# Moving the last FFN pair, the first-layer chunks and the value projections between the head slots of a transformer block kernel

## The chip, the cores and the metric

The kernel runs on one NeuronCore of a Trainium2 chip. Its engines run side by side, each in its own program order, and wait for one another by semaphores: TensorE (PE, with its weight loads shown apart as PEld), VectorE (DVE), ScalarE (ACT), GpSimd (POOL) and SyncE (SP), which here issues the DMA transfers. The metric is the device time of one execution in microseconds; less is better.

## What is computed

The input x has 16 batches of 512 tokens with 256 features. Each batch is normalised, and attention and a feed-forward network with weights of +1 and -1 are added to x:

```python
xn = _layernorm(x, axis=-1)
# attention, 8 heads of width 128
q = einsum('bim,mhd->bhid', xn, wq); k = einsum('bim,mhd->bhid', xn, wk)
v = einsum('bim,mhd->bhid', xn, wv)
q = rope(q); k = rope(k)
s = einsum('bhid,bhjd->bhij', q, k) / 128
s = s - 1e30 * mask                       # causal, i < j
o = einsum('bhij,bhjd->bhid', softmax(s), v)
attn = einsum('bhid,hdm->bim', o, wo)
# FFN, 512 -> 1024 -> 1024 -> 256
h = concatenate([xn, -xn], axis=-1)
h = relu(s0 * (h @ where(k0, 1, -1))) * 2
h = relu(s1 * (h @ where(k1, 1, -1))) * 2
ffn = s2 * (h @ where(k2, 1, -1))
out = x + attn + ffn
```

## The kernel before

The work is cut into 128 slots, one per batch and head; slot g has batch b = g // 8 and head h = g % 8. Below, "slot h" means the slot of head h in each batch. The slots are a software pipeline. In slot g the kernel computes the four score rows of head g with their softmax (`score_row`, L553), projects q and k of head g + 1 (`project_qk`, L508), applies the probabilities of head g - 1 to the values (`attend`, L618) and projects the result of head g - 2 to the output (`project_o`, L652).

A score row takes this way: PE multiplies (L558), DVE adds the mask and finds the least value (L561), ACT takes the exponential and its sum (L566), DVE the reciprocal (L568), POOL scales the row (L569). At the end of a slot `turn` (L573) lets DVE transpose the four rows in blocks (z, L578); SP stores them to a bounce buffer in DRAM (L335) and loads them back in another order as pT (L341, four transfers), which `attend` of the next slot reads. POOL also rotates q and k: multiplication of the swapped halves swq and swk with the sine table (L440) and addition into qT and kT (L442). The next slot's first score row waits for kT, the last POOL instruction of the chain.

The products of the projections and of the second FFN layer use seven products in the place of eight for a 2 by 2 split (`seven_products`, L464). They need differences of the operand's blocks: T1 to T4 of xn (`make_ts`, L398) and of the first layer's result (`add_h0`, L704, four POOL subtractions L708 per chunk). The two PSUM tiles pa and pb of such a product are accumulated in steps; ACT copies their state between steps to ca, cb and cu (L482, L487, L491), and the later steps on the same tile wait for these copies.

The FFN of a batch has three parts. The first layer (`ffn0`, L675) makes eight 128-row tiles, two for each of four chunks. ACT writes relu of it to h0r (L699). `split_h0` (L710) splits a chunk in a high part h0h, cast by ACT (L713), and a low remainder h0l, subtracted by DVE (L714), once for the plain blocks (PLAIN) and once for the four differences (SUMS). The second layer (`ffn1`, L718) runs in four pairs of seven products with 56 matmuls each, over weights w1 that lie in DRAM as two parts: part 0 (A11, A12, S1, A22; 1024 KB) is read by the first two steps of a pair and part 1 (S2, S4, A21; 768 KB) by the rest. From the second batch on both are loaded again for each pair (`load_w1`, L166). h0r of chunks 0 and 2 lies in the buffer of part 0, h0r of chunks 1 and 3 in that of part 1, so a chunk and a weight part wait for each other. The third layer (`ffn2`, L749) adds a finished pair to y, the PSUM sum that also takes the outputs of the heads.

The values v are projected in four steps a batch (`project_v`, L531): two groups of four heads with two token parts each.

Before the change the special slots are these. Slot 0 runs the last pair (3) of the batch before, and at its end chunks 0 and 1 of the first layer. Slot 1 runs chunks 2 and 3 and value step (0, 1). Slot 2 runs value step (1, 0), the third layer of pair 3 of the batch before, the `store` (L657) of that batch and the normalisation of the next batch's x. Slots 3, 5 and 6 run pairs 0, 1 and 2, and the slots after them the third layer of these (slots 4, 6 and 7). The next batch's x is transposed in slot 3, sent to DRAM in slot 4 (`carry_xn_out`) and brought back in slot 5 (`carry_xn_back`). Value step (1, 1) is in slot 4 and step (0, 0) of the next batch in slot 7.

The order of instructions on PE, SP and POOL is the program order, written by hand in `slot`, `slot_of_head_0` and `slot_of_head_1`: a generator such as `project_qk` stops at each `yield`, and `some(gen, n)` and `rest(gen)` place its next steps between the score rows. The order on DVE and ACT is set by a planner, which `behind` ties to a slot's rows. `begin` (L829) issues a slot's transfers on SP.

## Time and profile before

| what | value |
|---|---|
| median of two runs | 2250.07 us (2248.95 to 2251.2) |
| profiled execution, own time | 2253.46 us |
| its span, first to last instruction | 2251.6 us |
| PE, DVE, ACT, POOL busy | 2109.5, 1526.3, 1365.8, 1280.9 us |
| mean granted TensorE clock | 0.984 |
| DMA traffic | 455.55 MB, mean 202 GB/s |
| mean slot lengths, slots 0 to 7, batches 2 to 14 | 19.7, 20.6, 15.9, 18.9, 14.1, 16.0, 18.0, 14.7 us |
| one batch | 137.9 us |

The span is the time from the first to the last instruction of the one execution that was traced. A slot's length is the time from its first score matmul (128x128, L558) to that of the next slot, read from PE's timeline. Busy time of PE counts matmuls with modelled ends, so a busy PE may still run below its peak. In the waits of PE the two largest totals are 47.3 us for the copy ca_v in 42 places and 29.5 us for the load of w1 in 17 places.

### The profile page before, as it was taken

To read this page: it belongs to the slowest core of one execution; us is meant where nothing else is said; L and a number is where in the kernel's file an instruction comes from. 1 tells how busy PE (TensorE), PEld (TensorE's weight loads), DVE (VectorE), ACT (ScalarE), POOL (GpSimd) and SP (SyncE) were. 2 spreads that over 40 slices of the span, in tenths; PEclk is the share of its full clock that TensorE was granted. 3 is DMA by queue.
4 is the path that set the end of the run, shared out by engine and by line. 5 is a ranking of instruction groups with operands and counts; after the bars stand their busy time and mean duration, and the time that the engine had idled before them with its cause. 6 is when DMAs were issued, how large, how long until landed. Compare 5 with 4: busy or idle time off the path is not lost.

```text
span 2251.6 us, 34771 instructions
## 1 busy us (share of the span) xinstructions
PE 2109.5 (94%) x11392; PEld 1792.9 (80%) x11392; DVE 1526.3 (68%) x3774; ACT 1365.8 (61%) x2884; POOL 1280.9 (57%) x1332
## 2 busy tenths in 40 slices
PE   7899999989999899998999989999899999989998
PEld 4677878878788787787878878788787877878787
DVE  7877667676666766667667676766767666676664
ACT  6656565565656656566566566656556565565663
POOL 6546456465555656456465565655556456465652
PEclk9999999999999999999999999999999999999999
DMA  4684957749477584775847658486684957748575
GB/s 146 216 259 128 277 159 223 235 140 264 140 237 229 150 255 143 236 216 158 271 146 234 215 163 274 131 258 188 181 252 128 281 160 224 237 143 250 161 223 161
DMA packets 214596, 455.55 MB, mean 202 GB/s; under 512 B 30992, under 2 KB 150800, under 8 KB 206224
## 3 DMA queue, kind: packets, MB, share of 16 engines
q1 hardware_dynamic: 213392, 452.42, 66.3%
q8 instruction: 91, 1.49, 0.3%
q10 hardware_dynamic: 1024, 0.92, 0.1%
q14 instruction: 89, 0.73, 0.1%
HBM read 339.22 MB, written 114.03 MB: 201 GB/s over the span
## 4 chain that ended last, share of the span: by engine, by line
PE 67%; DVE 15%; ACT 6%; DMA 6%; issue 3%; POOL 1%; SPq 0%; ACTq 0%; DVEq 0%; POOLq 0%
PE pa_h L725 11%; PE y L644 11%; PE po L599 10%; PE pb_h L725 8%; PE s L558 7%; PE pa_qk L517 7%; PE pb_qk L517 6%; DMA w<-w_dram 5%; DVE h0l L714 4%; PE ph L692 3%; PE pa_v L541 3%; DVE z L578 2%; DVE p L561 2%; PE pb_v L541 1%; ACT h0r L699 1%
## 5 line engine op out<-in xcount | busy, mean ns | idle before, releaser
L569 POOL TENSOR_SCALAR p<-p,rl 128x128 f32<-128x128 f32 (+3 forms) x512 | 319.7, 627 | 594.6 <-DVE rl L568 593.1
L558 PE MATMUL s<-kT,qT 128*128 128x128 f32 (+3 forms) x1024 | 364.0, 437 | 1.7 <-DVE least L561 1.7
L566 ACT ACTIVATE p<-p,least 128x128 f32<-128x128 f32 (+3 forms) x512 | 287.9, 563 | 119.2 <-DVE least L561 113.7
L440 POOL TENSOR_TENSOR swq<-swq,sin_sb 128x512 f32<-128x512 f32 x127 | 192.1, 1513 | 270.2 <-ACT swq L435 268.4
L725 PE MATMUL pa_h<-h0h,w 128*128 128x256 f32 x1024 | 294.6, 322 | 33.5 <-DMA w<-w_dram 29.5
L599 PE MATMUL po<-pT,v 128*128 128x256 f32 (+1 forms) x1536 | 300.7, 345 | 2.9 <-DMA pT<-bounce_p 2.9
L599 PEld LDWEIGHTS po<-pT,v 128*128 128x128 f32 x1536 | 268.2, 191 | 34.4 <-issue 3.3
L561 DVE CUSTOM_DVE_ANT_0 p<-s,causal 128x128 f32<-128x128 f32 (+3 forms) x512 | 245.6, 484 | 71.3 <-PE s L558 68.1
L578 DVE STREAM_TRANSPOSE z<-p 128x128 f32<-128x128 f32 (+3 forms) x512 | 237.3, 489 | 52.2 <-POOL p L569 51.3
L708 POOL TENSOR_TENSOR h0r<-h0r 128x256 f32<-128x256 f32 x256 | 232.4, 933 | 53.9 <-ACT h0r L699 50.1
L725 PE MATMUL pa_h<-h0l,w 128*128 128x256 f32 x1024 | 257.1, 286 | 0.0
L644 PE MATMUL y<-wo,oT 128*128 128x256 f32 x1024 | 253.1, 392 | 0.0
L714 DVE TENSOR_TENSOR h0l<-h0r,h0h 128x1024 fp32r<-128x1024 f32 (+1 forms) x128 | 189.8, 1483 | 91.3 <-ACT h0h L713 91.2
L725 PEld LDWEIGHTS pa_h<-h0h,w 128*128 128x128 f32 x1024 | 196.9, 192 | 65.8 <-issue 16.1
L644 PEld LDWEIGHTS y<-wo,oT 128*128 128x128 f32 x1024 | 202.4, 199 | 30.4 <-issue 0.5
L725 PE MATMUL pb_h<-h0h,w 128*128 128x256 f32 x768 | 212.8, 313 | 0.0
L725 PEld LDWEIGHTS pa_h<-h0l,w 128*128 128x128 f32 x1024 | 198.0, 193 | 16.0 <-issue 15.2
L558 PEld LDWEIGHTS s<-kT,qT 128*128 128x128 f32 x1024 | 184.7, 193 | 21.5 <-DVE least L561 2.3
L626 ACT COPY oT<-po 128x512 f32<-128x512 f32 x127 | 74.5, 586 | 189.4 <-PE po L599 189.4
L725 PE MATMUL pb_h<-h0l,w 128*128 128x256 f32 x768 | 189.3, 283 | 0.0
L434 ACT COPY swq<-q 64x512 f32<-64x512 f32 x126 | 78.2, 621 | 175.5 <-DVE q L525 173.8
L442 POOL TENSOR_TENSOR qT<-qT,swq 128x512 f32<-128x512 f32 x127 | 168.8, 1329 | 10.0
(132 smaller groups left out, 4644.4 us busy)
## 6 DMA issues: line engine op xcount, KB each, us to landing
bounce_p<-z SPq DMA_DIRECT2D x128, 640.0 KB, 3.5
pT<-bounce_p SPq DMA_DIRECT2D x512, 160.0 KB, 4.0
w<-w_dram SPq DMA_DIRECT2D x60, 1024.0 KB, 6.8
w<-w_dram SPq DMA_DIRECT2D x120, 448.0 KB, 5.4
w<-w_dram SPq DMA_DIRECT2D x60, 768.0 KB, 8.5
wv<-wv_dram SPq DMA_DIRECT2D x30, 896.0 KB, 6.2
wo<-in_L_attn_wo_dram SPq DMA_DIRECT2D x128, 128.0 KB, 5.4
w<-w_dram SPq DMA_DIRECT2D x60, 256.0 KB, 7.1
```

The costliest lines, as they stand in the source:

```text
L440: engine.tensor_tensor(sw, sw, sin_sb, ALU.mult)
L517: nc.tensor.matmul(out_, w[:, place], of_xn(b, x), skip_group_check=True, **marks)
L558: nc.tensor.matmul(ps[:, :n], qT[:, ts(ic, P)], kT[:, :n], start=True, stop=True)
L561: reduced = nc.vector.tensor_tensor_reduce(out=p, in0=ps[:, :n], in1=causal[:, T - n :], scale=1.0, scalar=3e38, op0=ALU.add, op1=ALU.min, ...
L566: raised = nc.scalar.activation(p, p, AF.Exp, bias=least, scale=-1.0, accum_out=l)
L569: nc.gpsimd.tensor_scalar(p, p, rl, 1.0, ALU.mult, ALU.mult)
L578: behind(nc.vector.transpose(zs[:, :, block(ic, 0) : block(ic + 1, 0), :].rearrange("p j c a -> p c j a"), p.rearrange("p (c j a) -> p c j ...
L599: nc.tensor.matmul(po[:, (ics[0] - first) * P : (ics[-1] + 1 - first) * P], v[:, jc], pT[:, :, at[0] : at[-1] + 1 : max(at[-1] - at[0], 1) ...
L644: nc.tensor.matmul(ys[b][c // 2][:, c % 2, :], lhsT[:, ts(c, P)], rhs, start=(y_done[b][c] == 0 and c % 2 == 0), stop=(y_done[b][c] == N_Y ...
L708: nc.gpsimd.tensor_tensor(r[:, out_], r[:, p], r[:, q], ALU.subtract)
L714: behind(nc.vector.tensor_tensor(lo, r, hi.bitcast(F32), ALU.subtract), reduced)
L725: nc.tensor.matmul(out_, w1s[b, i, place][:, c], t[:, c, x], start=start and not c + n, stop=stop and c == NC - 1 and n == 1, skip_group_c ...
```

## The change

The last pair runs in slot 7 of its own batch, so that pairs are in slots 3, 5, 6 and 7 and the third layer always in the slot after. The first layer's chunks 0 and 1 run in slot 0 between the score rows, chunk 2 in slot 1 and chunk 3 in slot 2; their POOL differences now stand between the score rows too. The value steps are in slots 0, 1, 2 and 4. The store of a batch moves from slot 2 to slot 1. Normalisation, transposes, transfer out and transfer back of the next batch's x come a slot later (slots 3, 4, 5 and 6), its T differences are made in the second half of slot 6, and the load of x two batches on moves from slot 3 to slot 4. Part 0 of the first pair's weights is issued in the `turn` of slot 2 as before; part 1 is issued by `begin` of slot 3.

The diff:

```diff
--- before.py
+++ after.py
@@ -817,13 +817,14 @@
         nc.sync.dma_start(wv7_dram[gv], wv7s[0, gv])
 
 
+    PAIR_SLOTS = (3, 5, 6, 7)
+    assert NPAIR == len(PAIR_SLOTS)
+
     def pair_of(g):
 
         b, h = divmod(g, H)
-        if h == 0 and b:
-            return b - 1, NPAIR - 1
-        if h in (3, 5, 6) and b < B:
-            return b, (3, 5, 6).index(h)
+        if h in PAIR_SLOTS and b < B:
+            return b, PAIR_SLOTS.index(h)
         return None
 
     def begin(g):
@@ -843,12 +844,10 @@
             load_w2(*now)
         if b == B:
             return
-        if h in (4, 6, 7):
-            i = (4, 6, 7).index(h) + 1
-            if b == 0:
-                store_w1(i)
-            elif h != 6:
-                load_w1(b, i, 1)
+        if b == 0 and h in (4, 6, 7):
+            store_w1((4, 6, 7).index(h) + 1)
+        elif b and h in (3, 4):
+            load_w1(b, h - 3, 1)
         if b == 0:
             if g == 1:
                 store_wv7(0)
@@ -858,16 +857,15 @@
                 store_wv7(1)
             if h in (3, 4, 6):
                 load_k1((3, 4, 6).index(h) + 1)
-        if h == 3:
+        if h == 4:
             if b + 2 < B:
                 xs[b + 2] = load_x(b + 2)
-        elif h == 4:
             x_sums[b] = load_x_sum(b)
-            if b + 1 < B:
-                carry_xn_out(b + 1)
         elif h == 5 and b + 1 < B:
+            carry_xn_out(b + 1)
+            load_wv7(b + 1, 0)
+        elif h == 6 and b + 1 < B:
             carry_xn_back(b + 1)
-            load_wv7(b + 1, 0)
 
     def store_w2(i):
         nc.sync.dma_start(w2_dram[i], w2s[0, i].bitcast(F32))
@@ -879,13 +877,13 @@
         if n < B:
             if h == 1 and n == 1:
                 ln_stats(n, xs[n], ic, reduced)
-            elif h == 2:
+            elif h == 3:
                 ln_normalize(n, xs[n], ic, reduced)
-            elif h == 3:
+            elif h == 4:
                 transpose_xn(n, ic, reduced)
-            elif h == 6 and ic:
-                for i in range(ic - 1, ic if ic < NT - 1 else NT):
-                    make_ts(n, i, reduced)
+            elif h == 6 and ic > 1:
+                for i in range(2):
+                    make_ts(n, 2 * (ic - 2) + i, reduced)
             elif h == 7 and ic >= NT - 2:
                 split_xn(n, ic - (NT - 2), reduced, raised)
         if h == 5 and n + 1 < B:
@@ -915,102 +913,109 @@
 
         b = g // H
         begin(g)
-        tile = ffn1(b - 1, NPAIR - 1)
+        l2 = ffn2(b - 1, NPAIR - 1)
         if b == B:
-            rest(tile)
+            rest(l2)
             project_o(g - 2)
             attend_by_halves(g - 1)
             return
         l0 = [ffn0(b, f) for f in range(NF0)]
         qk = project_qk(g + 1)
+        v = project_v(b, 0, 0)
         some(qk, 1)
         for ic in range(NT):
-            reduced, _ = score_row(g, ic)
+            reduced, raised = score_row(g, ic)
             if ic == 0:
                 some(qk, 1)
-                project_o(g - 2)
+                rest(l2)
                 some(qk, 1)
             else:
-                some(tile, 1)
                 if ic > 1:
                     some(qk, 1)
+                    add_h0(b, ic - 2)
+                    split_h0(b, ic - 2, PLAIN, reduced, raised)
+                if ic < NT - 1:
+                    rest(l0[ic - 1], l0[NC + ic - 1])
+                else:
+                    some(v, 1)
         rest(qk)
+        project_o(g - 2)
+        some(v, 1)
         turn(g, reduced)
-        rest(tile)
+        split_h0(b, 0, SUMS, reduced, raised)
+        rest(v)
         attend(g - 1)
-        for c in range(2):
-            rest(l0[c], l0[NC + c])
-        for c in range(2):
-            add_h0(b, c)
-            split_h0(b, c, PLAIN)
-        if b == 1:
-            make_w2(NPAIR - 1, reduced)
         return l0
 
-    def slot_of_head_1(g, l0):
-        b = g // H
+    def slot_of_head_1_or_2(g, l0):
+
+        b, h = divmod(g, H)
         begin(g)
         if b == B:
-            rest(ffn2(b - 1, NPAIR - 1))
             project_o(g - 2)
             store(b - 1)
             return
+        c = h + 1
         qk = project_qk(g + 1)
-        v = project_v(b, 0, 1) if b else iter(())
+        v = project_v(b, *((0, 1) if h == 1 else (1, 0))) if b or h == 2 else iter(())
         some(qk, 1)
         for ic in range(NT):
             reduced, raised = score_row(g, ic)
-            between_rows(b, 1, ic, reduced, raised)
-            if ic in (0, 2):
-                split_h0(b, ic // 2, SUMS, reduced, raised)
+            between_rows(b, h, ic, reduced, raised)
             if ic == 0:
+                if b or h == 2:
+                    split_h0(b, h, SUMS, reduced, raised)
+                else:
+                    split_h0(b, 0, SUMS, reduced, raised)
                 some(qk, 1)
-                rest(l0[2])
+                rest(l0[c])
                 some(qk, 1)
             elif ic == 1:
-                rest(l0[NC + 2])
+                rest(l0[NC + c])
+                if b and h == 1:
+                    project_o(g - 2)
+                    store(b - 1)
             else:
+                if b == 0 and h == 1 and ic == 2:
+                    split_h0(b, 1, SUMS, reduced, raised)
                 some(qk, 1)
                 some(v, 1)
-            if b == 0 and ic == 2:
-                scale_w7_qk(g + 2, raised)
+            if ic == 2:
+                add_h0(b, c)
+                split_h0(b, c, PLAIN, reduced, raised)
+                if b == 0:
+                    scale_w7_qk(g + 2, raised)
             elif b == 0 and ic == 3:
                 sum_w7_qk(g + 2, reduced)
         rest(qk)
-        if b:
+        if h == 2:
             project_o(g - 2)
         rest(v)
-        if b:
+        if b and h == 1:
             load_wv7(b, 1)
-        else:
-            make_w7_v(1, reduced, raised)
-            ln_deviations(1)
-        turn(g, reduced)
-        rest(l0[3], l0[NC + 3])
-        for c in range(2, NC):
-            add_h0(b, c)
-            split_h0(b, c, PLAIN)
+        turn(g, reduced, ((b, 0, 0),) if b and h == 2 else ())
+        if h == 2:
+            split_h0(b, c, SUMS, reduced, raised)
         attend(g - 1)
+        if b == 0:
+            if h == 1:
+                make_w7_v(1, reduced, raised)
+                ln_deviations(1)
+            else:
+                make_w1(0, reduced, raised)
 
     def slot(g):
         b, h = divmod(g, H)
         begin(g)
         qk = project_qk(g + 1) if g + 1 < N_SLOTS else iter(())
-        tile = ffn1(*pair_of(g)) if pair_of(g) else iter(())
-        before = pair_of(g - 2 if h == 2 else g - 1)
-        l2 = ffn2(*before) if before else iter(())
-        v = iter(())
-        if h in (2, 4):
-            v = project_v(b, 1, h // 2 - 1)
-        elif h == H - 1 and b + 1 < B:
-            v = project_v(b + 1, 0, 0)
+        now, before = pair_of(g), pair_of(g - 1)
+        tile = ffn1(*now) if now else iter(())
+        v = project_v(b, 1, 1) if h == 4 else iter(())
         some(qk, 1)
         for ic in range(NT):
             reduced, raised = score_row(g, ic)
             between_rows(b, h, ic, reduced, raised)
-            if h == 2 and ic in (1, 2):
-                split_h0(b, 1 + ic, SUMS, reduced, raised)
-            if g + 2 < H:
+            if b == 0 and g + 2 < H:
                 if ic == 2:
                     scale_w7_qk(g + 2, raised)
                 elif ic == 3:
@@ -1018,27 +1023,20 @@
             if ic == 0:
                 some(qk, 1)
                 if before:
-                    some(l2, 2 * NT)
+                    rest(ffn2(*before))
                 else:
                     project_o(g - 2)
                 some(qk, 1)
-                continue
-            if ic == 1:
-                rest(l2)
-                if h == 2 and b:
-                    store(b - 1)
             else:
-                some(qk, 1)
-            some(tile, 1)
-            if ic > 1:
-                some(v, 1)
+                if ic > 1:
+                    some(qk, 1)
+                some(tile, 1)
+                if ic > 1:
+                    some(v, 1)
         rest(qk)
         loads = ()
-        if b and h == 2:
-            loads = ((b, 0, 0), (b, 0, 1))
-        elif b and pair_of(g):
-            i = pair_of(g)[1] + 1
-            loads = ((b, i, 0), (b, i, 1))[: 2 if h == 5 else 1]
+        if b and now and now[1] + 1 < NPAIR:
+            loads = [(b, now[1] + 1, n) for n in range(1 if h == 3 else 2)]
         turn(g, reduced, loads)
         if before:
             project_o(g - 2)
@@ -1046,12 +1044,10 @@
         attend(g - 1)
         if h == 5 and b + 2 < B:
             ln_deviations(b + 2)
-        if b == 0:
-            if h == 2:
-                make_w1(0, reduced, raised)
-            if pair_of(g):
-                i = pair_of(g)[1]
-                make_w2(i, reduced)
+        if b == 0 and now:
+            i = now[1]
+            make_w2(i, reduced)
+            if i + 1 < NPAIR:
                 make_w1(i + 1, reduced, raised)
 
     E = mybir.EngineType
@@ -1074,8 +1070,8 @@
         for g in range(1, N_SLOTS + 2):
             if g % H == 0:
                 l0 = slot_of_head_0(g)
-            elif g % H == 1:
-                slot_of_head_1(g, l0)
+            elif g % H < 3:
+                slot_of_head_1_or_2(g, l0)
             else:
                 slot(g)
 # ---- launch: one core; inputs and outputs as the reference has them ----
```

## The prediction

> **What bounds the kernel now.** I read the summary and the chain of work that ended last, then cut one middle batch (its eight slots, each from the first 128x128 score matmul to the next slot's) with the view of stretches, then read the DMA issues and the engines' timelines inside the slots that are too long.
>
> ```profile
> span 2251.6 us, 34771 instructions
> ...
> PE 67%; DVE 15%; ACT 6%; DMA 6%; issue 3%; POOL 1%; SPq 0%; ACTq 0%; DVEq 0%; POOLq 0%
> ```
>
> The matrix engine (PE) leads two thirds of the chain; the rest is slots in which another engine or a load leads. Eight rows, slots 0 to 7 of one batch (columns: stretch, length, busy time of PE, PEld, DVE, ACT, POOL with counts, granted clock, DMA share, GB/s):
>
> ```profile
> core 0: us, PE busy (x) PEld busy (x) DVE busy (x) ACT busy (x) POOL busy (x), PEclk, DMA share, GB/s
> 1001.10:1020.80 19.70, 19.70 (x115) 17.24 (x115) 11.22 (x27) 12.97 (x27) 10.95 (x12) 1.00 0.52 149
> 1020.80:1041.60 20.80, 18.23 (x73) 14.24 (x72) 15.93 (x30) 14.45 (x28) 17.72 (x20) 0.92 0.27 80
> 1041.60:1057.50 15.90, 14.55 (x74) 11.89 (x73) 15.16 (x33) 10.24 (x21) 10.09 (x10) 1.00 0.50 153
> 1057.50:1075.80 18.30, 16.27 (x100) 14.18 (x99) 10.41 (x30) 9.79 (x21) 7.45 (x8) 1.00 1.02 276
> 1075.80:1089.90 14.10, 14.10 (x74) 11.96 (x73) 7.98 (x25) 8.28 (x19) 7.62 (x8) 1.00 1.02 329
> 1089.90:1105.90 16.00, 16.00 (x99) 14.22 (x98) 11.18 (x35) 9.69 (x21) 9.87 (x10) 1.00 0.84 244
> 1105.90:1123.60 17.70, 17.70 (x116) 16.10 (x115) 12.65 (x31) 9.75 (x21) 7.71 (x8) 1.00 0.76 245
> 1123.60:1138.30 14.70, 14.24 (x73) 11.96 (x72) 9.59 (x27) 9.46 (x21) 8.34 (x8) 1.00 0.70 220
> ```
>
> Against these stands what the matmuls alone need, summed from the chain's pieces: every slot has projections 3.02, scores 2.16, attention 2.17 and output 1.73, 9.08 us together; a pair of the second layer adds 6.67, of the third 1.90, a chunk of the first 1.86, a values step 3.01. So slots 0 to 7 need 19.5, 15.8, 14.0, 15.8, 14.0, 15.8, 17.7, 14.0, or 126.4 us, and over thirteen batches they take 19.7, 20.6, 15.9, 18.9, 14.1, 16.0, 18.0, 14.7: 137.9. The excess to be won lies in slots 1 (4.8), 2 (1.9), 3 (3.2) and 7 (0.7). Slots 1 and 2 are full on DVE, ACT and POOL; slot 3 waits for weights while the DMA engines are full (share 1.02).
>
> **The change, slot by slot.** Matmuls move and their total stays 126.4. What each slot becomes is decided by what ends last in it. I take the places from the two instruction orders and the durations from the trace.
>
> Slot 7 gets the pair (6.67) and loses values (3.01): 17.7 of matmuls, the make-up of slot 6, which runs at 18.0 on average with its weight waits. So 18.0: **+3.3**. Its loads are now issued 3.1 us ahead of the slot as slot 6's are; with 0.5 MB more queued before them I leave the cost inside that mean.
>
> Slot 6: the four T subtractions on DVE, now behind both h1l instructions (which end 16.1 after row 0), are 0.4 us each while POOL rests; the second pb_qk product reads the last one at 17.7 instead of 17.2. **+0.45**.
>
> Slot 0 needs 17.7 of matmuls (pair out, values and third-layer pair in). But POOL's four subtractions of chunk 0 now stand behind swk, which ends 10.8 after row 0 (slot 6's row, same place), and ACT's cast of their result stands ahead of the copy cu_v, for which the last values product waits.
>
> ```profile
> L708 POOL TENSOR_TENSOR h0r<-h0r 128x256 f32<-128x256 f32 x256 | 232.4, 933 | 53.9 <-ACT h0r L699 50.1
> ```
>
> Four take 2.9 (0.73 when DVE leaves POOL alone) to 3.7 (this mean): 14.2. Cast 1.03, cu_v 0.36: 15.7. Then PE has 0.43 + 2.17 + 0.87 + 0.86 left: 20.1, with bounds 19.8 and 20.6. **+0.5**.
>
> Slot 1: the other chunk's casts and subtractions leave it, as does chunk 3, matmuls 13.9. POOL again has four subtractions, now ahead of the row-3 scaling and of kT, and row 0 of the next slot needs kT. POOL's undisturbed run is slot 4's:
>
> ```profile
> 1079.92 1.54 POOL L440 TENSOR_TENSOR swq<-swq,sin_sb 128x512 f32<-128x512 f32 x1 [2.17 <-ACT swq L435]
> ...
> 1085.97 1.27 POOL L442 TENSOR_TENSOR kT<-kT,swk 128x512 f32<-128x512 f32 x1
> ```
>
> That is 4.1 after row 0 to 11.5. In slot 1 swq starts 1.2 later (cast 1.03 and subtract 1.2 to 1.6 of the sums stand ahead of q), the row-2 scaling waits 0.7 for ACT, which copies values first, and the subtractions put 3.3 in: kT ends at 16.7, with contention 17.2. Take 17.0 against 20.6: **-3.6** (bounds -4.3, -3.0). Slot 2 is the same without that wait: 16.2 against 15.9, **+0.3**; normalisation (4 x 0.62) and the store (2 x 0.67) leaving DVE buy nothing, since POOL is late next. In slots 3 and 4 PE hides the normalisation and the transposes: DVE has 10.4 and 8.0 us in 18.3 and 14.1. Without that cover they would cost their 2.5 and 1.8. The store in slot 1 lies on DVE before POOL needs its result: nothing, at most 0.7.
>
> Slot 3 decides. Before, both parts of the first pair's weights are issued behind the bounce store, in front of pT. Now part 0 stays there and part 1 (768 KB, read by the third step, S2) is issued at the start of slot 3, behind four pT, w7, wo and w2 on SP. The issues of this place, with time to landing:
>
> ```profile
> w<-w_dram SPq DMA_DIRECT2D x1, 1024.0 KB, 6.6
> w<-w_dram SPq DMA_DIRECT2D x1, 768.0 KB, 9.7
> bounce_p<-z SPq DMA_DIRECT2D x1, 640.0 KB, 3.5
> pT<-bounce_p SPq DMA_DIRECT2D x4, 160.0 KB, 8.5
> ...
> w<-w_dram SPq DMA_DIRECT2D x1, 256.0 KB, 10.5
> ```
>
> The 256 KB of w2, issued at 1063.2, need 10.5 us: they land at 1073.7, last of the row, 10.5 after part 0 (1056.6 + 6.6 = 1063.2). Put last, part 1 closes the same bytes, so it lands about then (9.7 to 10.7 in the batches I read). Part 0 gates the pair's first matmul already:
>
> ```profile
> 1063.35 0.36 PE L725 MATMUL pa_h<-h0h,w 128*128 128x256 f32 x1 [2.02 <-DMA w<-w_dram]
> ```
>
> The S2 step comes 5.0 us after it, so PE waits 5.0 more. Lower bound 0 (part 1 overtakes), upper 5.7. The bounce itself goes out later against the next row 0, 0.5 ahead instead of 1.3: +0.8. And the clock: after waits over 2.3 us in slots 1 and 3 the trace grants half speed for 3.4 us:
>
> ```profile
> 785.00:789.00 4.00, 4.00 (x19) 3.39 (x19) 0.66 (x2) 0.59 (x1) 1.10 (x2) 0.57 1.08 203
> ```
>
> PE is busy throughout that row at a clock of 0.57. Slot 3 is 1.6 us longer in the six batches of fifteen that have it (0.64 of the mean). A 5 us wait should have it always: +1.0. Slot 3: 18.9 + 0.8 + 5.0 + 1.0 = 25.7, **+6.8**.
>
> The Trainium skill, "TensorE: Matmul & The Clock Gate", Part 1, puts the half rate after an idle window of about 3.4 us. By that rule slot 3's present 2 to 3 us waits should not trigger it, though they do; the new wait passes either mark. "DMA: Bandwidth & Descriptors", section "Queues, rings and completion order", speaks against my reading: completion is not first in, first out per issuing engine. If that let part 1 land early, slot 3 would lose its 5.0 and 1.0 and the sum would be the first rival's.
>
> Sum per batch: 3.3 + 0.45 + 0.5 - 3.6 + 0.3 + 6.8 = +7.7; fifteen batches (the first makes its weights on the chip) +116. First batch and tail: matmuls and vector work keep their totals, I take 0, with bounds -8 (the pair's 6.7 us that PE runs after the last slot now precede the last bounce, which may hide them, and about 1 of store) and +12 (three more slots of the first batch that lose 4 as slot 1 does). The profiled execution took 2253.5 (span 2251.6), so 2369; the median of the runs is 3.4 lower: 2366. With POOL's subtractions a little quicker than their mean, as slot 1's last rows are (0.73), I forecast **2360**.
>
> **Rivals.** (1) Part 1 lands in time: no 5.0 and no 1.0. Per batch +1.7, in all +25: 2276. For it: the engines may serve two transfers at once. Against: x, issued 8.7 after row 0, lands only when w2 has. 15%. (2) The other side: part 1 in time, and the scheduled order lets POOL finish kT before PE ends its own work, so slots 0, 1, 2 run at 17.9, 14.3, 14.3 as slot 4 does (14.1 for 14.0). The price is -1.8 - 6.3 - 1.6 = -9.7, with +3.75 of slots 6, 7 and +0.8: -5.1, or -77: 2173. It decides once kT ends 2.7 us earlier in slot 1; the four subtractions alone are 2.9. 8%. (3) Part 1 late but slots 0 to 2 free: -9.7 + 3.75 + 6.8 = +0.9: 2263. 10%. (4) Worse: half speed also after the waits in slots 0 and 1 (1.6 each) in most batches, +40: 2400. 12%. The forecast's own case has 55%.
>
> **How the numbers follow.** About 2% is what this kernel's measurement can tell from no change. Slower by over 2% (above 2295): forecast, rival 4 and a sliver of 1, 0.70. Within 2%: rivals 1 and 3, 0.22. Faster: rival 2, 0.08. The range reaches down past rivals 1 and 3 to 2255 and up over 4 to 2405. The forecast's case alone: 2315 to 2385.
>
> **What would show it.** In the new profile: slot 3 near 25 us, with PE's wait before L725 on w<-w_dram growing from 29.5 to 90 us or more and a second one of some 5 us in each batch; slots 1 and 2 ending on kT of POOL (L442); L541 of slot 0 waiting for cu_v; slot 7 near 18. If the L725 waits stay at 2 us and slots 1 and 2 take under 15, the forecast is wrong through slot 3's queue and POOL's chain, in that order.

## The result, and the profile after

The changed kernel takes 2331.54 us (median of two runs, 2329.38 to 2333.7) against 2250.07 us: a ratio of 1.036 (95% interval 1.032 to 1.041), so it is slower by 3.6%. The forecast was 2360 with a range of 2255 to 2405. The profiled execution took 2329.38 us, 75.9 more than that of before.

The head and the chain of work of the changed kernel's summary page:

```profile
span 2327.6 us, 34736 instructions
...
PE 2124.4 (91%) x11392; PEld 1795.6 (77%) x11392; DVE 1479.5 (64%) x3774; ACT 1345.2 (58%) x2884; POOL 1257.0 (54%) x1332
...
PE 51%; POOL 18%; DMA 11%; issue 7%; ACT 6%; DVE 4%; SPq 1%; POOLq 0%; ACTq 0%; DVEq 0%
```

PE runs the same 11392 matmuls, but its share of the chain falls from 67% to 51%. POOL's goes from 1% to 18%, and that of the DMA transfers from 6% to 11%. The vector engines got no busier; their work came to stand in front of PE. The eight slots of one batch (batch 7, counted from 0), with the columns of the prediction's table:

```profile
core 0: us, PE busy (x) PEld busy (x) DVE busy (x) ACT busy (x) POOL busy (x), PEclk, DMA share, GB/s
1033.90:1056.30 22.40, 19.64 (x89) 16.08 (x88) 11.94 (x27) 12.68 (x26) 15.44 (x16) 0.92 0.37 107
1056.30:1073.00 16.70, 14.70 (x65) 11.34 (x64) 12.62 (x29) 11.40 (x24) 10.90 (x12) 1.00 0.41 133
1073.00:1089.20 16.20, 14.76 (x64) 11.43 (x64) 10.04 (x27) 10.94 (x23) 11.04 (x12) 1.00 0.39 117
1089.20:1112.10 22.90, 17.82 (x98) 15.63 (x99) 12.49 (x33) 9.99 (x22) 7.47 (x8) 0.93 0.82 264
1112.10:1126.10 14.00, 14.00 (x73) 12.01 (x73) 9.60 (x29) 8.25 (x19) 7.55 (x8) 1.00 0.78 223
1126.10:1142.10 16.00, 16.00 (x99) 14.22 (x99) 11.09 (x34) 9.67 (x21) 9.84 (x10) 1.00 0.83 258
1142.10:1161.10 19.00, 18.19 (x116) 15.93 (x115) 11.90 (x31) 9.56 (x21) 7.64 (x8) 1.00 0.89 276
1161.10:1178.80 17.70, 17.70 (x116) 16.11 (x115) 10.85 (x28) 10.79 (x23) 8.47 (x8) 1.00 0.61 179
```

Slots 4, 5 and 7 are full of matmuls. Slots 0 and 3 lose the most, 2.8 and 5.1 us of rest, and both show a clock below 1. Means over batches 1 to 14, beside the forecast's terms:

| slot | before | after | measured change | forecast |
|---|---|---|---|---|
| 0 | 19.7 | 21.75 | +2.1 | +0.5 |
| 1 | 20.6 | 16.7 | -3.9 | -3.6 |
| 2 | 15.9 | 16.2 | +0.3 | +0.3 |
| 3 | 19.0 | 21.4 | +2.4 | +6.8 |
| 4 and 5 | 30.1 | 30.0 | -0.1 | 0 |
| 6 | 18.0 | 18.8 | +0.8 | +0.45 |
| 7 | 14.7 | 17.7 | +2.9 | +3.3 |
| batch | 138.1 | 142.5 | +4.5 | +7.7 |
| first batch (slots 0 to 7) | 142.9 | 157.8 | +14.9 | 0 |
| from slot 127's row 0 to the end | 31.6 | 29.35 | -2.2 | 0 |

Fourteen batches at +4.5 are +63; with the first batch, the tail and the last batch (+0.9 up to slot 127) this gives the 76 by which the span grew.

Two waits make slot 0 and slot 3. From the table of PE's waits (engine, line and what it waited for: us in all, times, longest), first the one that the kernel before has too, then the changed kernel's three largest:

```profile
PE pa_h L725 <- DMA w<-w_dram: 29.5, 17, 2.9
...
PE pa_h L725 <- DMA w<-w_dram: 55.0, 30, 3.7
PE pa_v L541 <- ACT cu_v L491: 44.0, 30, 2.8
PE s L558 <- POOL kT L442: 26.9, 30, 1.5
```

The wait for kT is 1.52 us at the end of slot 1 and 0.27 at the end of slot 2, in every batch. Slot 2 rests longer before that: 0.77 us for ca_v and 0.39 for cu_qk.

**Slot 0.** POOL's, ACT's and PE's timelines inside the slot that begins at 1033.86:

```profile
1043.19 2.00 POOL L440 TENSOR_TENSOR swk<-swk,sin_sb 128x512 f32<-128x512 f32 x1
1045.16 3.67 POOL L708 TENSOR_TENSOR h0r<-h0r 128x256 f32<-128x256 f32 x4
```

```profile
1048.87 1.05 ACT L713 CAST h0h<-h0r 128x1024 fp32r<-128x1024 f32 x1 [2.14 <-POOL h0r L708]
1049.82 0.36 ACT L491 COPY cu_v<-pa_v 128x256 f32<-128x256 f32 x1
```

```profile
1050.23 1.20 PE L541 MATMUL pa_v<-wv,tt 128*128 128x256 f32 x2 [2.76 <-ACT cu_v L491]
```

This is the chain that the prediction named. POOL's four subtractions end 15.0 us after row 0, ACT's cast of their result waits 2.14 us for them, cu_v stands behind the cast, and PE rests 2.76 us for cu_v. It does so in all 15 batches.

**Slot 3.** SP's issues and PE's third step, in the slot that begins at 1089.2:

```profile
1088.69 0.32 SPq L335 DMA_DIRECT2D bounce_p<-z  x1
1089.05 0.43 SPq L169 DMA_DIRECT2D w<-w_dram  x1
1092.15 1.74 SPq L341 DMA_DIRECT2D pT<-bounce_p  x4
1094.00 0.38 SPq L140 DMA_DIRECT2D w<-w_dram  x1
1094.47 0.38 SPq L195 DMA_DIRECT2D wo<-in_L_attn_wo_dram  x1
1094.90 0.42 SPq L186 DMA_DIRECT2D w<-w_dram  x1
1095.97 0.32 SPq L169 DMA_DIRECT2D w<-w_dram  x1
```

```profile
1096.05 0.36 PE L725 MATMUL pa_h<-h0h,w 128*128 128x256 f32 x1 [2.89 <-DVE xn L314]
...
1103.78 0.36 PE L725 MATMUL pa_h<-h0h,w 128*128 128x256 f32 x1 [2.18 <-DMA w<-w_dram]
```

The first L169 is part 0, the last is part 1. Part 0 lands 6.7 after row 0 and PE starts the pair 0.14 later; the row names a DVE instruction for this wait, which happens to end at the same moment and whose result the matmul does not read. Part 1 leaves SP 0.06 after part 0 has landed, lands 7.7 later, and PE waits a second time. Over 15 batches the first wait is 2.99 us on average (2.05 before) and the second 0.92.

### The profile page after: what moved, and what is told of

It reads as the page before. It is cut to its first block, busy times and chain, and to the rows that moved or that the text cites. A ratio compares the mean times of both kernels' runs of the same rounds, so it can differ in the third digit from the quotient of the medians.

```text
span 2327.6 us, 34736 instructions
## 1 busy us (share of the span) xinstructions
PE 2124.4 (91%) x11392; PEld 1795.6 (77%) x11392; DVE 1479.5 (64%) x3774; ACT 1345.2 (58%) x2884; POOL 1257.0 (54%) x1332
## 4 chain that ended last, share of the span: by engine, by line
PE 51%; POOL 18%; DMA 11%; issue 7%; ACT 6%; DVE 4%; SPq 1%; POOLq 0%; ACTq 0%; DVEq 0%
PE y L644 9%; PE pa_h L725 9%; DMA w<-w_dram 8%; PE po L599 7%; PE s L558 7%; POOL h0r L708 7%; PE pb_h L725 6%; PE pa_qk L517 5%; PE pb_qk L517 4%; POOL p L569 3%; POOL swk L440 3%; PE pa_v L541 2%; POOL swq L440 2%; POOL qT L442 2%; ACT h0h L713 2%
## 5 line engine op out<-in xcount | busy, mean ns | idle before, releaser
L569 POOL TENSOR_SCALAR p<-p,rl 128x128 f32<-128x128 f32 (+3 forms) x512 | 283.8, 557 | 643.5 <-DVE rl L568 618.1
L440 POOL TENSOR_TENSOR swq<-swq,sin_sb 128x512 f32<-128x512 f32 x127 | 198.4, 1562 | 376.0 <-ACT swq L435 376.0
L725 PE MATMUL pa_h<-h0h,w 128*128 128x256 f32 x1024 | 294.4, 321 | 64.5 <-DMA w<-w_dram 55.0
L561 DVE CUSTOM_DVE_ANT_0 p<-s,causal 128x128 f32<-128x128 f32 (+3 forms) x512 | 246.4, 484 | 128.5 <-PE s L558 125.1
L599 PE MATMUL po<-pT,v 128*128 128x256 f32 (+1 forms) x1536 | 310.3, 353 | 1.0 <-DMA pT<-bounce_p 1.0
L599 PEld LDWEIGHTS po<-pT,v 128*128 128x128 f32 x1536 | 276.1, 197 | 35.2 <-issue 2.2
L725 PEld LDWEIGHTS pa_h<-h0h,w 128*128 128x128 f32 x1024 | 201.5, 197 | 102.1 <-DVE rl L568 26.1
L725 PE MATMUL pa_h<-h0l,w 128*128 128x256 f32 x1024 | 261.7, 289 | 0.0
L644 PE MATMUL y<-wo,oT 128*128 128x256 f32 x1024 | 242.7, 380 | 0.0
L725 PE MATMUL pb_h<-h0h,w 128*128 128x256 f32 x768 | 217.2, 318 | 0.0
L644 PEld LDWEIGHTS y<-wo,oT 128*128 128x128 f32 x1024 | 192.7, 191 | 25.8
L725 PEld LDWEIGHTS pa_h<-h0l,w 128*128 128x128 f32 x1024 | 202.2, 198 | 13.1 <-issue 12.0
L568 DVE RECIPROCAL rl<-l 128x1 f32<-128x1 f32 x512 | 80.6, 158 | 178.9 <-ACT p L566 174.9
L725 PE MATMUL pb_h<-h0l,w 128*128 128x256 f32 x768 | 191.5, 285 | 0.0
L714 DVE TENSOR_TENSOR h0l<-h0r,h0h 128x768 fp32r<-128x768 f32 (+1 forms) x128 | 165.4, 1293 | 33.5 <-ACT h0h L713 32.9
L440 POOL TENSOR_TENSOR swk<-swk,sin_sb 128x512 f32<-128x512 f32 x127 | 183.3, 1443 | 0.0
```

What stands on the lines that cost most here:

```text
L440: engine.tensor_tensor(sw, sw, sin_sb, ALU.mult)
L561: reduced = nc.vector.tensor_tensor_reduce(out=p, in0=ps[:, :n], in1=causal[:, T - n :], scale=1.0, scalar=3e38, op0=ALU.add, op1=ALU.min, ...
L569: nc.gpsimd.tensor_scalar(p, p, rl, 1.0, ALU.mult, ALU.mult)
L599: nc.tensor.matmul(po[:, (ics[0] - first) * P : (ics[-1] + 1 - first) * P], v[:, jc], pT[:, :, at[0] : at[-1] + 1 : max(at[-1] - at[0], 1) ...
L644: nc.tensor.matmul(ys[b][c // 2][:, c % 2, :], lhsT[:, ts(c, P)], rhs, start=(y_done[b][c] == 0 and c % 2 == 0), stop=(y_done[b][c] == N_Y ...
L714: behind(nc.vector.tensor_tensor(lo, r, hi.bitcast(F32), ALU.subtract), reduced)
```

## The experiments

Each run is compared with the kernel before on the same chip. Slot lengths are means over batches 1 to 14, from PE's timeline.

| kernel | median us | ratio to before (95%) | slots 0, 1, 2, 3 |
|---|---|---|---|
| before | 2250.07 | 1 | 19.7, 20.6, 15.9, 19.0 |
| changed | 2331.54 | 1.036 (1.032 to 1.041) | 21.75, 16.7, 16.2, 21.4 |
| e1_part1_turn | 2320.11 | 1.029 (1.026 to 1.032) | 21.8, 16.7, 16.2, 19.9 |
| e2_part0_early | 2324.50 | 1.031 (1.029 to 1.034) | 22.0, 16.7, 16.2, 21.2 |
| e5_both_parts | 2259.64 | 1.006 (1.004 to 1.008) | 21.95, 16.7, 16.2, 16.1 |
| e6_before_part1 | 2289.80 | 1.021 (1.019 to 1.023) | 19.7, 20.5, 15.9, 21.7 |
| e3_cuv_first | 2304.21 | 1.022 (1.019 to 1.026) | 18.0, 18.9, 16.2, 21.4 |
| e8_cuv_sums | 2279.44 | 1.017 (1.014 to 1.019) | 18.0, 17.3, 16.4, 21.2 |
| e4_kt_first | 2300.35 | 1.021 (1.019 to 1.023) | 21.5, 15.0, 16.8, 20.2 |
| e7_best | 2176.38 | 0.971 (0.968 to 0.973) | 18.0, 15.6, 16.3, 16.1 |
| e9_first_batch | 2177.30 | 0.970 (0.967 to 0.973) | 18.0, 15.6, 16.3, 16.1 |

### Slot 3: one part of the weights early, the other, both

**e1_part1_turn** issues part 1 in the `turn` of slot 2 again, as soon as chunk 3's last remainder is made:

```diff
-        turn(g, reduced, ((b, 0, 0),) if b and h == 2 else ())
-        if h == 2:
-            split_h0(b, c, SUMS, reduced, raised)
+        turn(g, reduced, ((b, 0, 0), (b, 0, 1)) if b and h == 2 else (),
+             (lambda z: split_h0(b, c, SUMS, z, raised)) if h == 2 else None)
...
-        elif b and h in (3, 4):
-            load_w1(b, h - 3, 1)
+        elif b and h == 4:
+            load_w1(b, 1, 1)
```

The function given to `turn` is called behind the bounce store and ahead of the loads.

> The changed kernel with one part undone: part 1 of the first pair's weights is issued at the end of slot 2 again, behind the bounce store and part 0 and ahead of pT, as soon as DVE has made the last low remainder of chunk 3 (about 1.2 us into slot 3). Theory A (the forecast's step: the late part 1 is what slot 3 pays, 5.0 of wait and 1.0 of half clock): slot 3 goes from 21.4 to about 19.7 or less, 2305 us or under. Theory B (read from the changed kernel's trace: SP issues part 1 only when part 0 has landed, 6.2 to 7.6 us into the slot, it lands 6.5 to 8.1 later, and PE reaches the step 5.6 or, at half clock, 6.8 after part 0; so the late part 1 costs only the second waits, 0.9 us a batch on average): slot 3 loses 0.9, the wait for part 0 (mean 3.0) and the half clock stay, about 2318 us; with the two parts sharing the DMA engines part 0 may land up to 0.5 later, 2325.

Part 1 is now issued 1.2 after row 0 and lands at 8.3 to 11.1. The second wait is gone in every batch and the first one stays (mean 2.75). Slot 3 loses 1.5 us, of which 0.9 is the second wait; stretches of 3.41 us at half speed fall from 11 to 8 over 15 batches. That is theory B in kind and between the two theories in size.

**e2_part0_early** issues part 0 in the middle of slot 2 and leaves part 1 where the change put it:

```diff
             elif ic == 1:
-                rest(l0[NC + c])
+                rest(l0[NC + c]); load_w1(b if h == 2 else 0, 0, 0)
...
-        turn(g, reduced, ((b, 0, 0),) if b and h == 2 else ())
+        turn(g, reduced, ())
```

> The changed kernel with part 0 of the first pair's weights issued in the middle of slot 2 (behind the slot's first DMAs, about 5 us into it) in place of the end of slot 2; part 1 stays at the start of slot 3. Theory B (part 0's wait of 3.0 us and the half-speed stretch behind it of up to 1.7 are what slot 3 pays): the wait before the pair's first matmul goes, the pair starts at 4.0, its third step is reached at 9.5 and waits up to 2 us for part 1; slot 3 about 18 to 18.5, some 2280 us. If part 1 lands by 9.5 as well: slot 3 at 16.4, about 2255. Theory A (part 1's landing is bound to its place last in the queue, 10 us after the row): the third step waits 3 to 4 us, slot 3 near 20 to 20.5, about 2315.

Theory B's forecast for this run failed. Part 0 lands 2.6 to 4.5 us before slot 3 begins and its wait is gone, but the slot takes 21.2 instead of 21.4. PE's timeline in slot 3 (it begins at 1084.98):

```profile
1093.66 0.59 PE L558 MATMUL s<-kT,qT 128*128 128x512 f32 x1
1098.20 0.55 PE L725 MATMUL pa_h<-h0h,w 128*128 128x256 f32 x1 [3.95 <-DMA w<-w_dram]
```

PE reaches the third step 3 us sooner and waits there 3.43 us on average, because part 1, issued 5.7 to 6.8 us into the slot, still lands at 11.6 to 13.6. Here it stands on SP behind the four pT loads, which go out only when the bounce has landed (2.4 us into the slot). Half speed follows this wait in all 15 batches. So theory A's wait of 3 to 4 us came, and the late part 1 alone is enough to hold slot 3 where it is; part 0's wait had hidden that. By the medians the kernel gains 7 us, but its interval overlaps with the changed kernel's, and its profiled execution is no shorter (2327.7 us of span against 2327.6).

**e5_both_parts** joins the two edits: part 0 in the middle of slot 2, part 1 in its `turn`.

> The changed kernel with both parts of the first pair's weights early: part 0 in the middle of slot 2 as in e2_part0_early, part 1 behind the bounce store at the end of slot 2 as in e1_part1_turn. Theory (the two parts stand behind one another, so that taking one wait away only shows the other): neither the first nor the third step of the pair waits, slot 3 takes 16.4 to 17 us in place of 21.4, 2255 to 2270 us. Rival (what is left is the traffic of slot 3, and the waits go to pT or w2 instead): slot 3 at 18.5 or more, 2290 or more.

Neither step waits in any batch, slot 3 takes 16.1 us against 15.8 of matmuls, and the kernel gains 72 us on the changed one. Each edit alone gave 11 and 7 (by the ratios 3.0% of the time before against 0.7% and 0.5%, two gains whose intervals overlap with the changed kernel's). From the window view, slots 2 and 3 of one batch, and PE's waits for the weights over the whole run:

```profile
1047.70:1063.90 16.20, 14.76 (x64) 11.43 (x64) 10.05 (x27) 10.91 (x23) 11.05 (x12) 1.00 0.53 182
1063.90:1080.00 16.10, 16.07 (x98) 14.32 (x99) 12.78 (x33) 9.79 (x22) 7.78 (x8) 1.00 0.75 230
```

```profile
PE pa_h L725 <- DMA w<-w_dram: 9.1, 10, 2.0
```

The DMA share is 0.75 in slot 3, where the kernel before had 1.02: 1 MB moved into slot 2, which had room for it.

**e6_before_part1** puts the same step into the kernel before, alone:

```diff
+        elif b and h == 3:
+            load_w1(b, 0, 1)
...
-            loads = ((b, 0, 0), (b, 0, 1))
+            loads = ((b, 0, 0),)
```

> The kernel before with one part of the change alone: part 1 of the first pair's weights is issued at the start of slot 3, last of its DMAs but x. The forecast's size (5.0 of wait at the third step and 1.0 of half clock): slot 3 from 18.9 to 25, about 2340 us. What the changed kernel's trace says in its place (SP issues it when part 0 has landed, 5.2 to 6.6 us into the slot, it lands 6.5 to 7 later, and PE reaches the third step 5.6 after part 0): slot 3 gets 1 to 2 us longer, 2265 to 2282 us.

Slot 3 goes from 19.0 to 21.7, above what the trace's reading gave and under half of the forecast's 6.0. The second wait is 1.77 us on average, and 13 stretches of 3.41 us at half speed stand where there were 6. So the step costs 2.7 us a batch by itself.

### Slot 0: the cast ahead of cu_v

**e3_cuv_first** ties ACT's cast of chunk 0's differences behind the copy cu_v (`last_cu` holds the instruction of L491):

```diff
-        nc.scalar.copy(cu, pa[:, :n])
+        last_cu[0] = nc.scalar.copy(cu, pa[:, :n])
...
-        split_h0(b, 0, SUMS, reduced, raised)
+        split_h0(b, 0, SUMS, reduced, last_cu[0])
```

> The changed kernel with ACT's cast of chunk 0's four differences in slot 0 placed behind the copy cu_v instead of ahead of it. If that cast is what the last values product waits for: the wait of 2.76 us in slot 0 goes, and with it the half-clock stretch that slot 0 shows in 7 of 14 batches (1.67 each, 0.8 a batch); slot 0 goes from 21.7 to 18.1. Then POOL's subtractions of chunk 1, which stand behind kT, end some 3 us into slot 1, later than the cast of slot 1's first row wants them, and slot 1 gets 0.5 to 1.5 longer: net 2.0 to 3.1 a batch, 2285 to 2302 us. Rival (POOL's chain of 12 subtractions is the bound and slot 0 is only where it shows): slot 1 gives all but 1 us back, 2315 or more.

Slot 0 takes 17.98 us in every batch: 3.8 less, the wait and all half-speed stretches. Slot 1 gives 2.2 back, a little more than expected. ACT's and PE's timelines in slot 1 (it begins at 1045.54):

```profile
1048.40 1.04 ACT L713 CAST h0h<-h0r 128x1024 fp32r<-128x1024 f32 x1 [0.56 <-POOL h0r L708]
1049.35 0.36 ACT L491 COPY cu_qk<-pa_qk 128x256 f32<-128x256 f32 x1
```

```profile
1049.77 0.94 PE L517 MATMUL pa_qk<-tt,w 128*128 128x256 f32 x2 [2.06 <-ACT cu_qk L491]
```

It is slot 0's pattern again with chunk 1: a cast that waits for POOL, ahead of the copy that PE waits for.

**e8_cuv_sums** adds that the casts of chunks 1 and 2 come one score row later:

```diff
-                if b or h == 2:
-                    split_h0(b, h, SUMS, reduced, raised)
-                else:
-                    split_h0(b, 0, SUMS, reduced, raised)
+                if b == 0:
+                    split_h0(b, h if h == 2 else 0, SUMS, reduced, raised)
...
             elif ic == 1:
+                if b: split_h0(b, h, SUMS, reduced, raised)
```

> e3_cuv_first, and ACT's casts of the differences of chunks 1 and 2 one score row later in slots 1 and 2, behind cu_qk. If the 2.2 us that slot 1 gave back in e3_cuv_first came from the cast that waits for POOL's subtractions ahead of cu_qk: slot 1 returns from 18.9 to 16.7, 2270 to 2280 us. Rival (POOL's subtractions at the start of slot 1 delay its first scaling and the rotation by themselves): slot 1 stays at 18 or more, 2290 to 2305 us.

Slot 1 goes from 18.9 to 17.3: most of what it gave back was the cast ahead of cu_qk. It stays 0.6 above the changed kernel's 16.7, which POOL's later subtractions can account for; that part was not tested by itself.

### Slots 1 and 2: the subtractions ahead of kT

**e4_kt_first** moves POOL's four subtractions behind kT in both slots:

```diff
-                add_h0(b, c)
                 split_h0(b, c, PLAIN, reduced, raised)
...
-        rest(qk)
+        rest(qk); add_h0(b, c)
```

> The changed kernel with POOL's four subtractions of chunk 2 (slot 1) and chunk 3 (slot 2) placed behind the scaling of the last row and kT instead of ahead of them. Theory (slots 1 and 2 end on kT, which the subtractions put 3.3 to 3.6 us off): kT ends at about 13 us, slot 1 takes 14.1 to 14.5 instead of 16.7; the subtractions then reach 2 to 3 us into the next slot, the cast of its first row waits for them and puts q some 1.2 off, so slot 2 takes 14.1 to 14.8 instead of 16.2, and slot 3 is unchanged or up to 0.5 longer: 2 to 4 us a batch, 2270 to 2300 us. Rival (POOL's work is the bound over the three slots together, and its order only moves the loss): under 1 us a batch, 2318 or more.

The expectation held for slot 1 only, and there not in full: 15.0 instead of 16.7, where 14.1 to 14.5 were expected, with no wait for kT left. Slot 2 got longer (16.8), because the subtractions now reach into it and hold the cast of its first row. ACT and PE there, and PE at the start of slot 3, where the same happens with ca_qk:

```profile
1066.85 1.04 ACT L713 CAST h0h<-h0r 128x1024 fp32r<-128x1024 f32 x1 [1.07 <-POOL h0r L708]
1067.80 0.37 ACT L491 COPY cu_qk<-pa_qk 128x256 f32<-128x256 f32 x1
```

```profile
1068.22 0.70 PE L517 MATMUL pa_qk<-tt,w 128*128 128x256 f32 x2 [1.58 <-ACT cu_qk L491]
```

```profile
1084.06 0.70 PE L517 MATMUL pa_qk<-tt,w 128*128 128x256 f32 x2 [2.39 <-ACT ca_qk L482]
```

The unforeseen gain is in slot 3 (20.2). Part 0 leaves SP 2.3 us before row 0 in place of 0.15, and PE's rest moves from the weights to ca_qk. The loss is tied to POOL's position in both ways: ahead of kT it holds row 0, behind kT it holds the cast.

### The edits together, and the first batch

**e7_best** has e5's and e3's edits and e8's later casts, and moves the subtractions behind kT in slot 1 alone:

```diff
-                add_h0(b, c)
+                if h == 2: add_h0(b, c)
...
         rest(qk)
-        if h == 2:
-            project_o(g - 2)
+        if h == 2: project_o(g - 2)
+        else: add_h0(b, c)
```

> The changed kernel with the edits of e5_both_parts and e3_cuv_first, with POOL's subtractions of chunk 2 behind kT in slot 1 (those of chunk 3 stay ahead of kT in slot 2), and with ACT's casts of the differences of chunks 1 and 2 one score row later in slots 1 and 2, behind the copy cu_qk. If the waits found so far are all that there is: slot 0 18.0, slot 1 14.3 to 15.0, slot 2 16.2, slot 3 16.4 to 17, the rest as in the changed kernel: 131.5 to 132.7 a batch instead of 142.5, 2170 to 2190 us, faster than both kernels. Rival: the later casts put part 0's load, which needs chunk 2's buffer, and the rows of slots 1 and 2 off: 2200 to 2240 us.

It takes 2176.38 us, 3% less than the kernel before (ratio 0.971, 0.968 to 0.973). Slots 0 to 3 of one batch:

```profile
972.90:990.90 18.00, 18.00 (x89) 14.87 (x89) 11.08 (x27) 12.78 (x26) 12.71 (x14) 1.00 0.30 88
990.90:1006.50 15.60, 14.82 (x66) 11.35 (x65) 14.05 (x30) 10.99 (x23) 11.16 (x12) 1.00 0.62 193
1006.50:1022.80 16.30, 14.38 (x66) 11.40 (x64) 11.32 (x27) 11.61 (x25) 13.29 (x16) 1.00 0.56 183
1022.80:1038.90 16.10, 16.10 (x98) 14.34 (x99) 12.63 (x32) 9.68 (x22) 7.77 (x8) 1.00 0.78 231
```

PE is full in slots 0 and 3. Slot 1 is above its expected 14.3 to 15.0: PE rests 0.73 us there (0.44 for cu_qk, 0.29 for cu_v), and the rest of the 1.6 above its matmuls stands in no wait. In slot 2 PE waits 1.29 us for ca_v, which stands behind the moved cast (0.77 in the changed kernel), and 0.64 for kT. The batch takes 132.3 us against 126.4 of matmuls.

**e9_first_batch** is e7_best with the next batch's x brought back first in slot 6 of the first batch. It goes after the one large term that the prediction had put at nothing.

```diff
         if b == 0:
+            if g == 6: carry_xn_back(1)
...
-        elif h == 6 and b + 1 < B:
+        elif h == 6 and 0 < b < B - 1:
             carry_xn_back(b + 1)
```

> e7_best, and in slot 6 of the first batch the next batch's x is brought back first of the slot's DMAs, ahead of the stores of weights. The changed kernel loses 14.9 us in the first batch, 7.1 of them in its slot 6, where DVE makes the four T differences only after the seven sums of the last pair's weights. Theory (the loss is DVE's work on those weights, which the last pair now needs in slot 7 of its own batch): with x there earlier DVE makes the T differences first, slot 6 of the first batch goes from 24.8 to about 21, and slot 7, whose pair then waits for its weights, from 18.7 to 20 to 22: in all 0 to 3 us less. Rival (the late x is the cause): slot 6 at 20 to 21 and slot 7 unchanged, 4 us less.

Slot 6 of the first batch goes from 24.8 to 19.9 and slot 7 from 18.7 to 20.9, where the pair now waits for its own weights. PE's timeline in that slot 7:

```profile
163.05 0.35 PE L725 MATMUL pa_h<-h0h,w 128*128 128x256 f32 x1 [1.50 <-DVE w L270]
...
167.12 0.36 PE L725 MATMUL pb_h<-h0h,w 128*128 128x256 f32 x1 [0.87 <-DVE w L788]
```

The two slots together gain 2.7 us, and the time of the whole kernel does not tell them from nothing (2177.30 us and a ratio of 0.970, against 2176.38 and 0.971). Both theories are partly right for slot 6: the late x held DVE's order, and under it DVE's sums for the last pair's weights fill the place. For slots 4 and 5 of the first batch (+2.2 and +2.4) there was no run. The changed kernel's trace names what PE waits for there: in slot 4 2.33 us for DVE's step of a score row (L561; all rests of this slot were 1.47 before), in slot 5 4.19 for DVE's sums of weights (L788; 2.63 before). The granted clock is 0.91 in both, where it was 1.00. Why DVE comes later there was not tested.

## Why the prediction was right, and where it was not

The sign, the range and the likeliest case were right; by its steps:

- **What would bound each slot** was right: L541 waiting for cu_v in slot 0, kT of POOL at the end of slots 1 and 2, the weights in slot 3, matmuls in slot 7. e3, e5 and e4 took the waits of slots 0, 3 and 1 away, and these slots got 3.8, 5.3 and 1.7 us shorter. For slot 2 it is read from the trace alone: kT ends last there, but by 0.27 us only, and in e4, without that wait, the slot got longer.
- **Slots 1, 2 and 7** came out within 0.4 us of their terms (-3.9, +0.3, +2.9).
- **Slot 3** had the right direction and the wrong size: "PE waits 5.0 more" measured 0.92 on average, with a second wait in 9 batches of 15, and the half clock was granted in 11 batches, not all. So the slot took 21.4 and not 25.7, and the L725 waits on w_dram grew from 29.5 to 55.0 us, not to 90. Two sub-steps failed. First, "put last, part 1 closes the same bytes": it landed 6.5 to 8.1 us after part 0, not 10. Part 1 left when part 0 had landed, and w2, the last of the seven loads then under way, landed 1.8 us or more ahead of it. And the change takes the 512 KB of x out of this slot, which the prediction did not count. What x is worth shows in e6, where x still follows part 1: part 1 takes 8.2 us from issue to landing on average over the 13 batches with an x to load and 6.7 in the two without (7.1 in the changed kernel). Second, the third step comes 5.0 us after the first matmul in the kernel before, but 5.6 in the changed one, and 6.6 to 7.1 where the stretch after the first wait runs at half speed: that stretch hid most of the second wait. The step "+0.8" for the later bounce was right (part 0's wait grew by 0.94).
- **"After waits over 2.3 us"** is not when the kernel before runs at half speed. Slot 1 waits 2.42 us in all 15 batches, and 8 of them have the stretch; slot 3 has one after a wait of 1.95. The last section shows what decides.
- **Slot 0** was mis-sized the other way, +2.1 for +0.5. The terms as written (14.2, 1.03, 0.36 and 4.33) add up to 19.9, which is +0.2; the prediction puts 20.1. The chain was the named one, but swk took 2.00 us and the subtractions began at 11.3 and took 3.67, so cu_v ended at 16.3 and not 15.7. With what PE had left (4.44, put at 4.33) that makes 20.8; the half-speed stretch that follows the wait in 8 of 15 batches (1.67 each) is the other 0.9. The prediction had this stretch only in rival 4.
- **First batch and tail**: "I take 0", with +12 as the upper bound; they measured +14.9 and -2.2, together 0.7 over that bound. Slots 4, 5 and 6 carry 11.7 of the 14.9. What was missed for slot 6 is that the weights of the last pair, which DVE makes there, are now needed one slot later and not two, while the T differences of the next batch come behind them; e9 shows the two in each other's way. The cause in slots 4 and 5 stays open.
- **Slot 6**: +0.8 for +0.45, and the term that was named, the T differences, is 0.16 of it. PE's waits there grew from 0.16 to 0.60 us a batch: 0.16 for the T differences, 0.13 for the weights and 0.14 for the return of the next batch's x. The other 0.4 stands in no wait.

So the total is 28 us under the forecast partly by chance: slot 3 was 4.4 a batch too high, slot 0 and the first batch 1.6 a batch and 15 us too low.

Of the rivals, (1) falls with e2 and e6, which show that the late part 1 has a price by itself, with part 0 early (e2) and in the kernel before (e6). (2) and (3), with slots 0 to 2 at their floors, are false of the changed kernel, but e3, e4, e8 and e7 show the point from which they decide where the prediction placed it: POOL's subtractions, and besides them the casts that wait for these. (4), half speed behind new waits, came true in slot 0 and not in slot 1, whose wait was removed. The Trainium skill's rule from "DMA: Bandwidth & Descriptors" (section "Queues, rings and completion order"), that completion need not follow the order of issue, did not help: in all 15 batches of the changed kernel part 1 landed 1.8 us or more after w2, which was issued before it.

## What to carry to other kernels

When two transfers feed two steps of one chain, undoing one delay alone proves little: the two gave 0.7% and 0.5% of the time singly and 3.0% together. Price a transfer from the time at which it can leave, not from its place among the bytes; the cheap cure was to issue both parts sooner, part 0 in an earlier slot whose DMA share was 0.39. And where an in-order engine holds a copy that the critical engine waits for, look at what stands ahead of that copy and whom it waits for: in slots 0, 1, 2 and 3 the cast of one chunk or another did the harm in turn. Moving the casts (e8) gained 2.0% of the time, moving their producer in slots 1 and 2 (e4) 1.5%.

## What the runs showed of the hardware that was not expected

**The half-speed stretches lie on a fixed grid.** In each of eleven traces the stretches with a granted clock of 0.5 begin at multiples of 3.413 us from one another, to within 0.002 us over the whole run. Slot 0 of the changed kernel shows what it means, since its wait is 2.76 us in every batch. The window view of the changed kernel, cut along this grid; two windows around the wait of batch 7, and three around that of batch 8:

```profile
1046.88:1050.29 3.41, 0.65 (x4) 0.25 (x3) 1.44 (x3) 1.32 (x2) 3.41 (x4) 1.00 0.00 0
1050.29:1053.71 3.42, 3.42 (x9) 2.87 (x10) 2.46 (x3) 0.00 (x0) 3.34 (x4) 0.50 0.47 192
1190.24:1193.66 3.42, 2.21 (x10) 1.44 (x8) 2.29 (x4) 1.46 (x4) 3.34 (x4) 1.00 0.00 0
1193.66:1197.07 3.41, 1.85 (x10) 1.67 (x11) 2.55 (x4) 1.32 (x2) 3.41 (x4) 1.00 0.30 122
1197.07:1200.48 3.41, 3.41 (x19) 3.07 (x18) 1.39 (x5) 1.75 (x4) 2.41 (x4) 1.00 0.52 164
```

In batch 7 the whole wait falls into one window, PE is busy for 0.65 us of it, and the next window runs 9 matmuls at 0.50. In batch 8 the same wait is cut in two, PE is busy for 2.21 and 1.85, and the next window runs 19 at full clock. Over all full-speed windows from the first batch's end to slot 127 of the eleven traces, 154 were followed by a half-speed window, and PE had rested 1.81 us or more in each of them; 6319 were not, and PE had rested at most 1.97. So about 1.9 us of rest inside one such window decides, and a wait of 2 to 3 us costs its length, and 1.67 us more or not by where it falls. This is why equal batches differ by 1.67 us here. The Trainium skill, "TensorE: Matmul & The Clock Gate", Part 1, has the free-running window of 3413 ns, and these runs agree; its condition of an idle window is stricter than what they show, since PE was busy for up to 1.6 us of windows that were followed by half speed.

**No more than eight transfers of SP are under way.** In all eleven traces, with 1329 DMAs of SP each, none was issued while more than seven earlier ones had not landed; with just seven, 210 to 240 were. Part 1 at the start of slot 3 is the eighth behind part 0, and in 14 of 15 batches of the changed kernel it was issued 0.06 us after part 0's landing, with seven still under way. In e2_part0_early, where part 0 was long there, it went out 0.4 to 0.8 us after the issue before it. Whether this is a limit of the chip or of how the program's DMAs are tracked, the runs do not tell.
